# Query products of the second sequence: f32 replaced by three passes of split f32r parts that borrow the feed-forward's weight space

## The chip, the cores and the metric

One core of a Trainium2 chip runs the whole kernel. The metric is device time in microseconds of one execution, as the median of several runs. Times inside an execution come from the hardware profiler, counted from the first instruction. TensorE is called PE, VectorE DVE, ScalarE ACT, GpSimd POOL, and SyncE, which issues nearly all transfers, SP.

## The reference

Two transformer layers over two sequences of 512 rows of width 512, each layer an attention part and a feed-forward part with a layer norm behind each. What matters here is the attention of layer 0, a memory that is read, and the feed-forward behind it:

```python
q = (x @ Wq.T + bq).reshape(b, s, 32, 128)
q_sel = (elu(q) + 1.0)[:, :, ::4, :]                 # 8 heads are used
num = einsum('bshd,hde->bshe', q_sel, M)
den = einsum('bshd,hd->bsh', q_sel, z)[..., None] + 1e-6
out = repeat(num / den, 4, axis=2).reshape(b, s, 4096) @ Wo.T
x = layernorm(x + out)
# feed-forward of layer 0: weights that are ternary times a scale, width 1376
gate, up = (x / 128) @ w_gate.T, (x / 128) @ w_up.T
inter = trunc(clip(silu(gate) * up * 128, -128, 127))
x = layernorm(x + trunc(clip(inter @ w_down.T * 128, -128, 127)))
# layer 1: softmax attention with one head, then a gated feed-forward of width 1376
```

## The kernel before

Rows lie in eight tiles `xs[b][t]` of 128 rows, sequence b, tile t. Layer 0's attention goes in three stages on PE.

First, `queries(0, xt, h)` for eight heads: the rows of sequence 0 are transposed on PE (`first_rows`), and each head is four f32 products of 128x128 by 128x512 (`query_products`, L325). ACT takes the exponential (L361) and the positive part (L363) from PSUM, DVE joins them into `q` (L365).

Second, the rows of sequence 1 are transposed (`transposed`, L125) and `queries(1, xt1, h)` does the same for them. Between the heads lie the eight `fold(h)`: M and Wo of a head are multiplied in advance into `mw` (L387 to L390). The four parts of Wo that share a head are added first, by `sum_weights` (L380, L382), for heads 0, 3, 5, 7 on POOL and for the others on DVE. Column 511 of `mw` is `z`, so that one product gives both the numerator and the denominator.

Third, `read(b, t, ...)` for the eight row tiles: eight f32 products `po` (L401), a column `den` of each copied by ACT (L405), a reciprocal per four heads on DVE (L409). Three heads are scaled into `y` by ACT (L414) and added on POOL (L418), five are added to x on DVE (L423), and POOL adds the sum of the three (L427). Meanwhile the layer norm of the tile before is made: statistics on DVE, the root on POOL (L143, L144), `off` on DVE (L503), the application on ACT (L504).

In the same time the kernel proves that the feed-forward's weights are ternary. `check_up(c, a)` divides the gate (a = 0) or up half (a = 1) of chunk c by its scale into a tile `t` (ACT, L433) and compares it, multiplied again, with the weight (DVE, `compare`, L204). There are 22 of these; three follow each of the last five heads of sequence 1, and seven follow row tiles 0 to 2. `total` and `verdict` make a flag from the counts, on which PE branches at the start of the feed-forward. `divided(c, a)` (ACT, L433 too) writes the ternary weights `ts_up[c]` that the feed-forward multiplies with; chunks 0 to 2 are made during `read` and the rest in the feed-forward.

The weights come over SP's queue in program order: wq, x, m, wo, chunk 0, the rest of wo, chunks 1 to 10 (`gu`, 512 KB each, L237), wqkv, bqk, bv, wo1, bo (L310 to L315); a transfer that waits for its buffer holds back those queued after it. Only POOL keeps the program's order. The order on the other engines is found by a planner from priorities and its own estimate of costs; `tc.issue_after` forces an instruction behind another on its engine.

Layer 1 already multiplies in f32r with numbers split exactly into an upper part, a lower part and a difference (`row_parts`, `weight_parts`): three passes whose products are put together by ACT and DVE (`sum_up`, L1080 and L1081).

Of the kernel before, what the change touches and what calls it, by code (L numbers as in the profile page):

```python
# [19 lines left out]
P = 128  # L20
# [9 lines left out]
LAST = HID - 1  # L30
LENT = 3
# [5 lines left out]
def kernel(  # L37
# [34 lines left out]
    wqkv = const.tile([P, NK, 3 * D], F32, tag="wqkv", name="wqkv")  # L72
    bv = const.tile([P, D], F32, tag="bv", name="bv")
    wo1 = const.tile([D, HID], F32, tag="wo1", name="wo1")
    bo = const.tile([P, HID], F32, tag="bo", name="bo")
# [194 lines left out]

    wop = ctx.enter_context(tc.tile_pool(name="wop", bufs=6))
# [9 lines left out]
    with tc.tile_pool(name="a0w", bufs=1) as a0w, tc.tile_pool(name="a0", bufs=2) as a0:  # L281
# [27 lines left out]
        gus += up_weights(gu0_in, "0", range(1, len(CHUNKS)))  # L309
        nc.sync.dma_start(wqkv, wqkv_in.rearrange("(k p) f -> p k f", p=P))  # L310
        bqk = const.tile([D, 3], F32, tag="bqk", name="bqk")
        nc.sync.dma_start(bqk, bqk_in)
        nc.sync.dma_start(bv, bv_in.to_broadcast([P, D]))
        nc.sync.dma_start(wo1, wo1_in)
        nc.sync.dma_start(bo, bo_in.to_broadcast([P, HID]))  # L315
# [4 lines left out]
        mw = a0w.tile([D, NH, HID], F32, tag="mw", name="mw")  # L320
        nc.gpsimd.tensor_copy(mw[:, :, LAST], z)

# [8 lines left out]
        def first_rows(xt, t):  # L331

            pt = psum(f"pt_a00_{t}")
            for k in range(NK):
                done = nc.tensor.transpose(pt[:, ts(k, P)], xs[0][t][:, ts(k, P)], ident)
            pt = pt.rearrange("p (k t) -> p k t", k=NK)
            nc.scalar.copy(xt[:, :2, ts(t, P)], pt[:, :2])
            nc.vector.tensor_copy(xt[:, 2:, ts(t, P)], pt[:, 2:])
            return done

        def first_queries(pq, xt):

            done = first_rows(xt, 0)
            for t in range(NT):
                if t + 1 < NT:
                    with tc.issue_after(done.ins):
                        done = first_rows(xt, t + 1)
                with tc.issue_after(done.ins):
                    done = query_products(pq, xt, 0, ts(t, P))
            return done  # L350

        def queries(b, xt, h):

            pq = psum(f"pq_{b}_{h}")
            if b == h == 0:
                done = first_queries(pq, xt)
            else:
                done = query_products(pq, xt, h, slice(0, S))

            e = a0.tile([D, S], F32, tag="e", name=f"e_{b}_{h}")  # L360
            nc.scalar.activation(e, pq, AF.Exp, bias=bq[:, h : h + 1])  # L361
            r = a0.tile([D, S], F32, tag="r", name=f"r_{b}_{h}")
            nc.scalar.activation(r, pq, AF.Relu, bias=bq[:, h : h + 1])  # L363
            q = a0.tile([D, S], F32, tag="q", name=f"q_{b}_{h}", bufs=16)
            nc.vector.scalar_tensor_tensor(q, e, 1.0, r, ALU.min, ALU.add)  # L365
            qs[b].append(q)
            return done
# [17 lines left out]
        def fold(h):  # L385
            p = psum(f"pmw_{h}")
            nc.tensor.matmul(p, m[:, h, :], wos[h], start=True, stop=True)  # L387
            c = small.tile([P, 1], F32, tag="col", name=f"col_{h}", bufs=2)
            nc.scalar.mul(c, p[:, LAST:], -1.0)
            nc.scalar.activation(mw[:, h, :LAST], p[:, :LAST], AF.Identity, bias=c)  # L390

        def read(b, t, between):
# [3 lines left out]
            for h0 in range(0, NH, 4):  # L396
                four = []
                den = small.tile([P, 4], F32, tag="den", name=f"den_{b}_{t}_{h0}")
                for j in range(4):
                    po = psum(f"po0_{b}_{t}_{h0 + j}")  # L400
                    nc.tensor.matmul(  # L401
                        po, qs[b][h0 + j][:, ts(t, P)], mw[:, h0 + j, :],
                        start=True, stop=True,
                    )
                    nc.scalar.activation(  # L405
                        den[:, j : j + 1], po[:, LAST:], AF.Identity, bias=den_eps
                    )
                    four.append(po)
# [29 lines left out]

        def check_up(c, a):
            n = CHUNKS[c][1]  # L440
            w = gus[c][:, a].rearrange("p k i -> p (k i)")
            t = a0.tile([P, NK * P], F32R, tag="t", name=f"t_{c}_{a}")
            ternary(nc.scalar, t[:, : NK * n], w, inv_up[:, a : a + 1])
# [8 lines left out]
        qs = [[], []]  # L452
        xt = xtp.tile([P, NK, S], F32, tag="xt", name="xt_a00")
        with tc.issue_after(queries(0, xt, 0).ins):
            queries(0, xt, 1)
        for h in range(2, NH):
            queries(0, xt, h)
            if h == 4:
                sum_weights(nc.gpsimd, 0)
                turn_memory()  # L460
                sum_weights(nc.vector, 1)
            elif h == 6:
                xt1 = transposed(xs[1], "a01")
                sum_weights(nc.vector, 2)
        sum_weights(nc.gpsimd, 3)
        for h in range(NH):
            queries(1, xt1, h)
            if h == 0:
                sum_weights(nc.vector, 4)
                sum_weights(nc.gpsimd, 5)  # L470
                fold(0)
                fold(1)
                mx_up = largest(
                    [gus[0][:, a].rearrange("p k i -> p (k i)") for a in range(2)], "up"
                )
# [15 lines left out]
            if h >= 3:  # L491
                for _ in range(3):
                    check_up(*checks.pop(0))
        order = [(b, t) for b in range(B) for t in range(NT)]
# [11 lines left out]
        def divided(c, a):  # L506
            n = CHUNKS[c][1]
            if c not in ts_up:
                t = query_tile(f"tu_{c}").bitcast(F32R)
                ts_up[c] = t.rearrange("p a (k i) -> p a k i", k=NK)  # L510
                if n < P:
                    nc.gpsimd.memset(ts_up[c][:, :, :, n:].bitcast(F32), 0.0)
            ternary(nc.scalar, ts_up[c][:, a, :, :n], gus[c][:, a], inv_up[:, a : a + 1])

        ts_up, x2 = {}, []
        for i, (b, t) in enumerate(order):
            steps = read(b, t, lambda steps: norm_a0(i - 1, steps) if i else None)
            for _ in range((3, 2, 2, 0, 0, 0, 0, 0)[i]):
                check_up(*checks.pop(0))
            if i == 3:  # L520
                tot_up = total(counts, "up")
            elif i == 4:
                flag_up, eff_up = verdict(tot_up, sc_up, "up")
            if i in (3, 4, 5):
                for a in range(2):
                    divided(i - 3, a)
# [23 lines left out]
    with tc.tile_pool(name="f0", bufs=2) as f0:  # L550
# [52 lines left out]
        to_divide = [(c, a) for c in range(3, len(CHUNKS)) for a in range(2)]  # L603
# [71 lines left out]
        to_divide[2:2] = [None, None]  # L675
# [73 lines left out]

    BIG = 4096.0
    MAIN, CROSS = 1.0 + 1.0 / BIG, 1.0 / BIG
    UPPER = 1.0 - 2.0**-13
    cutp = ctx.enter_context(tc.tile_pool(name="cutp", bufs=2))  # L760

    def upper(h, src):
        return nc.scalar.activation(h, src, AF.Copy, scale=UPPER)
# [16 lines left out]
    def row_parts(src, parts):  # L780

        h, l, d = parts
        upper(h, src)
        nc.vector.tensor_sub(l, src, h.bitcast(F32))
        return nc.vector.scalar_tensor_tensor(
            d, l.bitcast(F32), -BIG, h.bitcast(F32), ALU.mult, ALU.add
        )

# [5 lines left out]

    def units(tile):
        return [tile[:, i, :] for i in range(tile.shape[1])]
# [28 lines left out]
    early = inter_tiles("early", F32R)  # L825
    room0 = units(early[0][2]) + units(early[1][2])
    room1 = units(early[0][1]) + units(early[1][1])
# [453 lines left out]
```

## Time and profile before

| what | us |
|---|---|
| median of 3 runs (471.8 to 799.53) | 472.01 |
| the profiled execution | 471.99 |
| its span, first to last instruction | 470.0 |
| PE busy | 463.0 |
| DVE busy | 327.9 |
| ACT busy | 268.1 |
| POOL busy | 114.4 |

The granted TensorE clock was 0.996 of full speed. Busy times of an engine overlap where its instructions are pipelined: a record's length is more than the step from one start to the next. The mean load of an engine over the span says little here, since the stages load the engines differently.

### The profile page before, as it was taken

The page shows a single profiled execution, that of the slowest core. Times are in us where ns is not written, and L with a number is a line of the kernel's source. Part 1 is how long each engine was busy: PE and PEld are TensorE (multiplying, and loading weights), DVE is VectorE, ACT ScalarE, POOL GpSimd, SP SyncE. Part 2 cuts the span into 40 slices and gives each one's busy share as a digit, 9 for nine tenths or more (in the row PEclk, how much of TensorE's full clock was granted, in tenths as well). Part 3 has the DMA queues.
Part 4 walks back from the last instruction along what each step waited for, and adds up shares of the span by engine and source line. Part 5 has one row for each costly group of instructions (what it writes and reads, how often), then busy time and mean ns, then how long its engine had stood idle before and what let it go on. Part 6 is the DMA issues. An engine that isn't in the chain of part 4 may idle for free.

```text
span 470.0 us, 5725 instructions
## 1 busy us (share of the span) xinstructions
PE 463.0 (99%) x1899; PEld 330.7 (70%) x1899; DVE 327.9 (70%) x622; ACT 268.1 (57%) x507; POOL 114.4 (24%) x141
## 2 busy tenths in 40 slices
PE   9999999999999999999999999999999999999995
PEld 8454444434478788888866568888888888888885
DVE  1265677767857677755988989986666767998633
ACT  3344799557556877645756743575644768532201
POOL 0343101566460090400348032000000000041101
PEclk9999999999999999999999999999999999999998
DMA  8999800000015000213192000000000000001011
GB/s 311 373 348 382 301 2 0 0 0 3 1 54 188 3 1 1 92 47 81 58 360 94 0 1 1 1 0 1 1 0 1 0 1 1 1 24 45 22 46 45
DMA packets 15187, 33.97 MB, mean 72 GB/s; under 512 B 3440, under 2 KB 4336, under 8 KB 15152
## 3 DMA queue, kind: packets, MB, share of 16 engines
q1 hardware_dynamic: 14864, 33.14, 19.6%
q8 instruction: 22, 0.36, 0.3%
q10 hardware_dynamic: 288, 0.36, 0.2%
q14 instruction: 13, 0.11, 0.1%
HBM read 31.40 MB, written 2.10 MB: 71 GB/s over the span
## 4 chain that ended last, share of the span: by engine, by line
PE 72%; ACT 7%; DVE 5%; issue 3%; POOL 0%; POOLq 0%; DVEq 0%; ACTq 0%
PE pm L1071 17%; PE pg_f L567 9%; PE pu_f L567 8%; PE pc L1071 8%; PE pdm L1159 7%; PE pd_f L622 4%; PE pdc L1159 4%; DVE x L423 4%; PE pqk L853 3%; PE po L401 2%; ACT y L414 2%; ACT t L433 2%; PE pv L866 2%; PE pot L949 1%; PE po L965 1%
## 5 line engine op out<-in xcount | busy, mean ns | idle before, releaser
L401 PE MATMUL po<-mw,q 128*128 128x512 f32 x128 | 57.1, 598 | 0.3 <-DVE mv_a L137 0.2
L325 PE MATMUL pq<-xt_a,wq 128*128 128x512 f32 (+1 forms) x152 | 56.9, 526 | 0.0
L143 POOL TENSOR_TENSOR rstd_f<-mv_f,ln_eps 128x1 f32<-128x1 f32 x15 | 4.4, 295 | 172.1 <-DVE mv_f L1174 130.2
L401 PEld LDWEIGHTS po<-mw,q 128*128 128x128 f32 x128 | 23.0, 189 | 32.1 <-issue 17.7
L325 PEld LDWEIGHTS pq<-xt_a,wq 128*128 128x128 f32 x152 | 26.2, 190 | 27.3 <-issue 26.2
L1071 PE MATMUL pm<-r,ugu 128*128 128x512 f32 x152 | 37.7, 389 | 0.0
L1071 PE MATMUL pm<-r,it_early 128*128 128x512 f32 x144 | 36.7, 392 | 0.0
L1071 PEld LDWEIGHTS pm<-r,ugu 128*128 128x128 f32 x152 | 28.5, 188 | 5.9
L1071 PEld LDWEIGHTS pm<-r,it_early 128*128 128x128 f32 x144 | 27.0, 188 | 6.0 <-issue 0.5
L423 DVE SCALAR_TENSOR_TENSOR x<-po,den,x 128x511 f32<-128x511 f32 x40 | 29.8, 745 | 1.9
L165 ACT ACTIVATE ta_f<-y_f,below_half 128x512 int8<-128x512 f32 (+1 forms) x22 | 15.9, 723 | 23.7 <-DVE y_f L155 23.3
L1081 DVE SCALAR_TENSOR_TENSOR ev_q<-pm,ev_q 128x512 f32<-128x512 f32 x27 | 18.6, 687 | 14.1 <-PE pm L1071 14.1
L418 POOL TENSOR_TENSOR y<-y,y 128x511 f32<-128x511 f32 x16 | 20.3, 1272 | 31.5 <-ACT y L414 30.8
L593 DVE SCALAR_TENSOR_TENSOR it_f<-tb_f,ta_f 128x512 fp32r<-128x512 int16 (+1 forms) x22 | 15.2, 690 | 16.3 <-ACT tb_f L166 16.3
L361 ACT ACTIVATE e<-pq,bq 128x512 f32<-128x512 f32 x16 | 11.1, 691 | 24.1 <-PE pq L325 21.7
L567 PE MATMUL pg_f<-xh,tu 128*128 128x512 f32 x88 | 24.7, 401 | 0.0
L1080 ACT ACTIVATE ev_q<-pc 128x512 f32<-128x512 f32 x27 | 16.0, 594 | 14.1 <-PE pc L1071 14.0
L435 POOL TENSOR_SCALAR td<-wd,inv_down 128x512 fp32r<-128x512 f32 x11 | 18.6, 1710 | 22.0 <-DVE inv_down L199 22.0
L567 PE MATMUL pg_f<-xl,tu 128*128 128x512 f32 x88 | 23.6, 390 | 0.0
L567 PE MATMUL pu_f<-xh,tu 128*128 128x512 f32 x88 | 23.6, 389 | 0.0
L567 PE MATMUL pu_f<-xl,tu 128*128 128x512 f32 x88 | 23.5, 389 | 0.0
L961 ACT ACTIVATE x<-x,off_f,rstd_f 128x512 f32<-128x512 f32 x7 | 5.7, 816 | 27.7 <-POOL off_f L960 27.7
(310 smaller groups left out, 1088.3 us busy)
## 6 DMA issues: line engine op xcount, KB each, us to landing
gu<-in_gu SPq DMA_DIRECT2D x20, 512.0 KB, 8.0
wo<-in_wo SPq DMA_DIRECT2D x16, 512.0 KB, 5.7
wd<-in_wd SPq DMA_DIRECT2D x20, 256.0 KB, 4.9
wq<-in_wq SPq DMA_DIRECT2D x8, 256.0 KB, 4.1
x<-in_x SPq DMA_DIRECT2D x7, 256.0 KB, 4.4
out<-x SPq DMA_DIRECT2D x7, 256.0 KB, 2.0
wqkv<-in_wqkv SPq DMA_DIRECT2D x1, 768.0 KB, 10.7
m<-in_m SPq DMA_DIRECT2D x1, 512.0 KB, 5.8
```

The source lines that it names most:

```text
L165: nc.scalar.activation(a[:n], y, AF.Relu, bias=below_half[:n])
L325: done = nc.tensor.matmul(pq[:, at], wq[h][:, k, :], xt[:, k, at], start=(k == 0), stop=(k == NK - 1),)
L401: nc.tensor.matmul(po, qs[b][h0 + j][:, ts(t, P)], mw[:, h0 + j, :], start=True, stop=True,)
L418: nc.gpsimd.tensor_add(ys[0][:, :LAST], ys[0][:, :LAST], y[:, :LAST])
L423: steps.append(nc.vector.scalar_tensor_tensor(x[:, :LAST], four[j][:, :LAST], d, x[:, :LAST], ALU.mult, ALU.add))
L435: eng.tensor_scalar(out, w, factor, None, ALU.mult)
L567: nc.tensor.matmul(pp[a], t[:, a, i % NK, :], x2[b][i], start=(i == 0), stop=(i == 2 * NK - 1),)
L622: nc.tensor.matmul(pd, inter[b][c][:, ts(t, P)], td[c].bitcast(F32R), start=(c == 0), stop=(c == last),)
L1071: nc.tensor.matmul(p, w, x, start=(left[id(p)] == begun[id(p)]), stop=(left[id(p)] == 1))
L1080: nc.scalar.activation(ev, pc, AF.Copy, scale=CROSS)
L1081: nc.vector.scalar_tensor_tensor(ev, pm, MAIN, ev, ALU.mult, ALU.add)
L1159: nc.tensor.matmul(p[:, :w], got[j // 4][1][kind][:, j % 4], down_parts[j][kind][:, cols], start=(j == 0 and kind == kinds[0]), stop=(j == ...
```

## The change

The query products of sequence 1 no longer run in f32. `second_rows(k)` transposes a block of rows as before and makes three f32r parts of it from PSUM: the upper part and its multiple by 4096 on ACT, the lower part and the difference on DVE. `split_query(h)` makes the three parts of a head's weights with `row_parts` (one ACT, two DVE operations). `second_queries(h)` then runs four f32r products into one PSUM bank (`pc`) and eight into another (`pm`); ACT and DVE put them together in `both`, and the ELU is made from that: an exponential on ACT, a `tensor_scalar` and a two-input operation on DVE.

The parts need room. The weights' parts lie in the buffers of chunks 1 to 9 of the feed-forward's weights, in the second half of `mw`, which is now two tiles `mws`, and for head 7 in a buffer of `xtp`. The rows' parts lie in `xtp`, in the `y` buffers and in the space of wqkv, wo1 and bo. So chunks 1 to 9 are loaded one after the other behind heads 1 to 6 of sequence 1 (`done_with`), and wqkv, bqk, bv, wo1 and bo after head 7.

The checks move: two follow each of heads 4 to 7, and fourteen follow row tiles 0 to 5. For chunks 0 to 3 the check's division is the one of `divided`, made once and kept. For chunks 4 to 10 the division of the up half runs on POOL. `total` and `verdict` come two row tiles later. `BIG`, `MAIN`, `CROSS`, `UPPER`, `upper`, `row_parts` and `units` are moved ahead unchanged, and the f32r tiles that layer 1 called `early` are called `spare`.

```diff
@@ tiles @@
+    early = [const.tile([P, 3, 512], F32R, tag="wqkv", name="e_wqkv")]
...
+    early += [const.tile([P, 1, 512], F32R, tag=tag, name=f"e_{tag}") for tag in ("wo1", "bo")]
@@ attention of layer 0 @@
-        gus += up_weights(gu0_in, "0", range(1, len(CHUNKS)))
-        nc.sync.dma_start(wqkv, wqkv_in.rearrange("(k p) f -> p k f", p=P))
+        gus += [None] * (len(CHUNKS) - 1)
+
+        def load_up(*chunks):
+            for c, gu in zip(chunks, up_weights(gu0_in, "0", chunks)):
+                gus[c] = gu
...
-        mw = a0w.tile([D, NH, HID], F32, tag="mw", name="mw")
-        nc.gpsimd.tensor_copy(mw[:, :, LAST], z)
+        room = [a0w.tile([P, 4, 512], F32R, tag="mw1", name="wp_mw")]
+        room = units(room[0])[:3]
+        for c in range(1, 10):
+            room += units(wffn.tile([P, 2, 512], F32R, tag=f"gu{c}", name=f"wp_{c}"))
+        wq_parts = [room[i : i + 3] for i in range(0, len(room), 3)]
+        done_with = {1: (1,), 2: (2, 3), 3: (4,), 4: (5, 6), 5: (7,), 6: (8, 9)}
+
+        def split_query(h):
+            with tc.issue_after(copies[2 * NT - 2].ins), tc.issue_after(copies[2 * NT - 1].ins):
+                row_parts(wq[h].rearrange("p k d -> p (k d)"), wq_parts[h])
+
+        def second_rows(k):
+            pt = psum(f"pt_a01_{k}")
+            for t in range(NT):
+                turned = nc.tensor.transpose(pt[:, ts(t, P)], xs[1][t][:, ts(k, P)], ident)
+            hx, l, d = x_parts[k]
+            upper(hx, pt)
+            big = a0.tile([P, S], F32, tag="t", name=f"hb_{k}")
+            nc.scalar.activation(big, hx.bitcast(F32), AF.Copy, scale=BIG)
+            nc.vector.scalar_tensor_tensor(l, pt, BIG, big, ALU.mult, ALU.subtract)
+            rows_done.append(nc.vector.tensor_sub(d, l.bitcast(F32), hx.bitcast(F32)))
+            return turned
+
+        def second_queries(h):
+            u, l, d = (w.rearrange("p (k d) -> p k d", k=NK) for w in wq_parts[h])
+            pc, pm = psum(f"pqc_{h}"), psum(f"pqm_{h}")
+            for k in range(NK):
+                nc.tensor.matmul(
+                    pc, d[:, k], x_parts[k][2], start=(k == 0), stop=(k == NK - 1)
+                )
+            for k in range(NK):
+                for i, w in enumerate((u, l)):
+                    nc.tensor.matmul(
+                        pm, w[:, k], x_parts[k][i],
+                        start=(k == i == 0), stop=(k == NK - 1 and i == 1),
+                    )
+            both = a0.tile([D, S], F32, tag="r", name=f"r_1_{h}")
+            nc.scalar.activation(both, pc, AF.Copy, scale=CROSS)
+            nc.vector.scalar_tensor_tensor(both, pm, MAIN, both, ALU.mult, ALU.add)
+            e = a0.tile([D, S], F32, tag="e", name=f"e_1_{h}")
+            nc.scalar.activation(e, both, AF.Exp, bias=bq[:, h : h + 1])
+            q = a0.tile([D, S], F32, tag="q", name=f"q_1_{h}", bufs=16)
+            nc.vector.tensor_scalar(q, both, bq[:, h : h + 1], 0.0, ALU.add, ALU.max)
+            nc.vector.scalar_tensor_tensor(q, e, 1.0, q, ALU.min, ALU.add)
+            qs[1].append(q)
...
         def check_up(c, a):
...
-            t = a0.tile([P, NK * P], F32R, tag="t", name=f"t_{c}_{a}")
-            ternary(nc.scalar, t[:, : NK * n], w, inv_up[:, a : a + 1])
+            if c < DIVIDED:
+                divided(c, a)
+                t = ts_up[c][:, a].rearrange("p k i -> p (k i)")
+            else:
+                t = a0.tile([P, NK * P], F32R, tag="t", name=f"t_{c}_{a}")
+                eng = nc.gpsimd if a else nc.scalar
+                ternary(eng, t[:, : NK * n], w, inv_up[:, a : a + 1])
...
+        for h in range(4):
+            split_query(h)
...
         for h in range(2, NH):
-            queries(0, xt, h)
+            done = queries(0, xt, h)
+            if h >= 5:
+                with tc.issue_after(elus[h - 1].ins):
+                    split_query(h - 1)
+            if h < 4:
+                for k in range(2):
+                    with tc.issue_after(done.ins):
+                        done = second_rows(2 * h - 4 + k)
             if h == 4:
                 sum_weights(nc.gpsimd, 0)
                 turn_memory()
-                sum_weights(nc.vector, 1)
+                with tc.issue_after(rows_done[-1].ins):
+                    sum_weights(nc.vector, 1)
             elif h == 6:
-                xt1 = transposed(xs[1], "a01")
-                sum_weights(nc.vector, 2)
+                with tc.issue_after(rows_done[-1].ins):
+                    sum_weights(nc.vector, 2)
         sum_weights(nc.gpsimd, 3)
+        load_up(10)
+        wq_parts.append(units(xtp.tile([P, NK, 512], F32R, tag="xt", name="wp_xt"))[:3])
         for h in range(NH):
-            queries(1, xt1, h)
+            second_queries(h)
+            load_up(*done_with.get(h, ()))
             if h == 0:
+                split_query(7)
                 sum_weights(nc.vector, 4)
                 sum_weights(nc.gpsimd, 5)
+                half_of_products()
...
-            if h >= 3:
-                for _ in range(3):
+            if h >= 4:
+                for _ in range(2):
                     check_up(*checks.pop(0))
+        wqkv = const.tile([P, NK, 3 * D], F32, tag="wqkv", name="wqkv")
+        nc.sync.dma_start(wqkv, wqkv_in.rearrange("(k p) f -> p k f", p=P))
...
         for i, (b, t) in enumerate(order):
             steps = read(b, t, lambda steps: norm_a0(i - 1, steps) if i else None)
-            for _ in range((3, 2, 2, 0, 0, 0, 0, 0)[i]):
+            for _ in range((2, 3, 2, 3, 2, 2, 0, 0)[i]):
                 check_up(*checks.pop(0))
-            if i == 3:
+            if i == 5:
                 tot_up = total(counts, "up")
-            elif i == 4:
+            elif i == 6:
                 flag_up, eff_up = verdict(tot_up, sc_up, "up")
-            if i in (3, 4, 5):
-                for a in range(2):
-                    divided(i - 3, a)
```

## The prediction

> **What bounds the kernel now.** I read the page's busy shares first, then TensorE's (PE's) order of time around the query products, then the order of time of VectorE (DVE), ScalarE (ACT) and GpSimd (POOL) in the stage behind them, then the table by stage. The page:
>
> ```profile
> span 470.0 us, 5725 instructions
> PE 463.0 (99%) x1899; PEld 330.7 (70%) x1899; DVE 327.9 (70%) x622; ACT 268.1 (57%) x507; POOL 114.4 (24%) x141
> ```
>
> PE is busy from end to end, so what counts is how many microseconds PE's own list takes, and where it is held back without looking idle. PE in order of time (start, length, line), second sequence's query products and the stages behind:
>
> ```profile
> 42.51 3.60 PE L325 MATMUL pq<-xt_a,wq 128*128 128x512 f32 x8
> 45.95 0.27 PE L184 MATMUL pmx_up<-ident,mx_up 128*2 128x128 f32 x1
> ...
> 68.88 3.60 PE L325 MATMUL pq<-xt_a,wq 128*128 128x512 f32 x8
> 72.31 35.47 PE L401 MATMUL po<-mw,q 128*128 128x512 f32 x80
> ...
> 130.65 1.50 PE L567 MATMUL pg_f<-xh,tu 128*128 128x512 f32 x4
> ```
>
> One head in f32 is eight records, and the next starts 3.44 us on (45.95 less 42.51). The stage that reads the memory (`read`, L401) runs from 72.31 to 130.65, 58.34 us. Its 64 f32 products are 0.86 us each (3.44 / 4), so 55.0, and 16 transposes add 1.74 (0.87 per eight records at L264): 56.8. So 1.5 us of that stage is PE being held. What holds it shows on DVE, one tile of rows:
>
> ```profile
> 91.94 0.20 DVE L503 TENSOR_SCALAR off<-mv_a,rstd_a 128x1 f32<-128x1 f32 x1
> 92.06 0.17 DVE L409 RECIPROCAL den<-den 128x4 f32<-128x4 f32 x1
> 92.34 0.75 DVE L423 SCALAR_TENSOR_TENSOR x<-po,den,x 128x511 f32<-128x511 f32 x1
> 95.36 0.18 DVE L409 RECIPROCAL den<-den 128x4 f32<-128x4 f32 x1 [2.28 <-ACT den L405]
> ...
> 99.27 0.20 DVE L503 TENSOR_SCALAR off<-mv_a,rstd_a 128x1 f32<-128x1 f32 x1
> 99.39 0.17 DVE L409 RECIPROCAL den<-den 128x4 f32<-128x4 f32 x1
> ```
>
> It is a loop of two engines: the reciprocal at 92.06 releases ACT (norm 0.7, three y, four den: 3.3 us), ACT releases the reciprocal at 95.36, DVE adds four heads and the statistics (4.0 us), and so on: 7.33 us a tile against PE's 6.87. In it DVE has one hole, the 2.28 us before 95.36 (2.13 in later tiles). POOL in the same tile:
>
> ```profile
> 92.11 1.27 POOL L427 TENSOR_TENSOR x<-x,y 128x511 f32<-128x511 f32 x1 [0.80 <-DVE x L423]
> 94.22 2.61 POOL L418 TENSOR_TENSOR y<-y,y 128x511 f32<-128x511 f32 x2 [0.85 <-ACT y L414]
> ```
>
> POOL works 4.6 us of 7.3 here, 3.9 of them tensor_tensor.
>
> **What the skill says.** The Trainium skill, SBUF — State Buffer, "Who interferes with whom": a DVE instruction with two SBUF inputs contends with a GpSimd instruction that reads SBUF, and the one that comes second waits for the whole of the first. The trace agrees for POOL's tensor_tensor:
>
> ```profile
> 25.27 1.21 DVE L380 TENSOR_TENSOR wo<-wo,wo 128x1024 f32<-128x1024 f32 x1
> 30.87 2.05 DVE L380 TENSOR_TENSOR wo<-wo,wo 128x1024 f32<-128x1024 f32 x1 [2.58 <-DMA wo<-in_wo]
> 30.58 1.26 POOL L382 TENSOR_TENSOR wos<-wo 128x512 f32<-128x512 f32 x1
> ```
>
> (first two from DVE, third from POOL): the second add takes 0.84 us more, until POOL ends at 31.84. Against POOL's tensor_scalar it agrees less: of eleven compares `junk_d` beside or near L435 the median is 0.75 and the worst 1.17 us. VectorE: DVE Perf Modes, "The perf-mode tier table": f32 tensor_scalar in SBUF has a 2× mode and two-input operations have none; here L155 takes 0.43 us, the two-input L593 0.69.
>
> **The change, part by part.** Back to back, a two-input DVE operation of 128x512 costs 0.61 us (starts of L365 and L380's neighbours at 26.41, 27.01, 27.61), an ACT pass 0.61, a compare 0.85 (75.77 to 76.61, its accumulator read included), a tensor_scalar 0.35.
>
> (1) PE. Removed: eight heads at 3.44 = 27.5. Added: eight heads of twelve single-pass products. The feed-forward runs eight such in 1.81 us and the twelve of the second layer's up product at 2.72 (the chain's 311.66 to 314.38); the weight load is 0.19 and fits in 0.227. 8 x 2.72 = 21.8. Saved: **5.75 us**. The 16 transposes of the second sequence move forward between heads 2 and 4 and stay 16. x of the second sequence is issued at 7.5 to 9.4 us and lands some 4.4 later, before head 2 ends at about 17.5, so the move costs 0.
>
> (2) Splits. Rows: four blocks of two ACT and two DVE operations, in place of four copies. Weights: eight heads of one ACT and two DVE. DVE stands idle for 2.25, 2.74 and 5.57 us between 10 and 22 us, and works 11.4 of 16.4 us from 24.4 to 40.8. Seven heads and the rows need 22 x 0.61 = 13.4, less two copies, 12.2; heads 0 to 3 and the rows (9.8) fall in the first hole. Cost 0. The adds of folded weights wait behind `rows_done` by perhaps 2 us; `fold` 2 and 3, the next users, come at about 47. If that cover went, PE would wait up to 2.
>
> (3) Second query stage. It begins on PE at 37.4 (33.93 + 3.44) and now lasts 21.8 + eight folds 6.9 + 0.4 = 29.1, to 66.5. DVE there: 8 x (0.61 + 0.35 + 0.61) = 12.6, eight compares 6.8, the rest of two sums 2.4, splits 2.4, small 0.8: 25.0, plus some 2 us of waits behind POOL's two sums (7.6 us long in all). 27 of 29: late, not over. ACT: eight passes for `pc`, eight exponentials, eight folds of 0.8, eight ternaries, one split: 21.6 of 29, where it was full before (8.60 of 8.60 from 56.0 to 64.6). Cost 0, bound 0 to 2.
>
> (4) Loads. SP now issues weight chunks 1 to 9 one by one behind heads 1 to 6, then wqkv, bqk, bv, wo1 and bo. Each waits for that head's products with everything on SP queued behind it. Chunks 8 and 9 go out near 61 us and need about 8 us at worst (the page's median of a full queue); tile 3 uses them near 90. wqkv is used at 236, wd is issued at 137.7 anyway. Cost 0.
>
> (5) Checks in `read`. Seven of 22 compares were left for this stage; now 14 are, in tiles 0 to 5 as 2, 3, 2, 3, 2, 2. From chunk 4 on, POOL forms the ternary of every second one: 1.70 us (L435, eight in 13.61), behind POOL's x add and ahead of its next y adds. A compare has two SBUF inputs; POOL holds tensor_tensor 3.9 of 7.3 us, so on the mean it waits 0.53 x 0.65 = 0.35: 1.2 us each. One of the fourteen falls in the long lead of tile 0 (5.85 us from 72.31 to the first reciprocal at 78.16); 13 x 1.2 = 15.6 against six holes of 2.2 = 13.2. Over: 2.4, all of it in the loop. Tile 3 has two POOL ternaries: 4.6 + 3.4 = 8.0 against 7.3, 0.7. Together **3.1 us given back**. Bounds: if every compare finds a hole, 0, and then PE's own 56.8 can also take back up to 1.5; if they fall badly, see rival B. POOL ternary beside a compare: between 0 and 0.4 of extra wait by L204's rows; I take 0.
>
> (6) ACT loses the six `divided` of tiles 3 to 5 and two later. In the trace they ran by 82 us, off the loop. 0. The verdict moves from tile 4 to 6, near 120; the branch needs it near 128. 0, at most 1 if PE reaches the sum first.
>
> Sum: -5.75 + 3.1 = -2.65. The profiled execution took 471.99 us, span 470.0 and 2.0 around it; the median of the runs is 472.01. 472.0 - 2.65 = **469.3 us**.
>
> **Rivals.** A, the full gain (0.2): the holes take everything. For it: five compares ran between 75.8 and 83 without stretching tiles 0 and 1 (7.17 and 6.73 us). Against: three on a tile need 2.55 of 2.2. 472.0 - 5.75 = 466.3.
>
> B, slower (0.3): POOL's ternary ends near 95.05 (93.4 + 1.65), just when the hole closes, and POOL's waiting y add starts at once. A compare set ahead of the reciprocal of 95.36 waits for that add until 96.35 and ends at 97.1: the loop is 1.75 us later. Six tiles make 10.5, net +4.75: 476.7. It decides from 3.3 such tiles (5.75 / 1.75). For it: POOL's list has this order. Against: the reciprocal and adds are older work, and a compare issued after them falls in the next hole.
>
> C, nothing gained (0.1): DVE becomes the bound of the query stage: 27 of 29 with more waits behind POOL, and banks fill. 2 us there plus the 3.1: 471.4.
>
> **How the numbers follow.** The forecast's own case has 0.4, from 467.5 to 471.5. The range 465.8 to 477.5 reaches from A with a little of the held 1.5 to B and leaves out some 2 in 10. Two per cent, 9.4 us, is about what a measurement of this kernel can tell from no change. A faster run by that needs more than the whole PE saving: 0.01. A slower one needs 15 given back, B on every tile together with C: 0.06. Same 0.93.
>
> **What would show it.** Right: query stage of eight heads at 2.72 spacing; first L401 product near 66.5; tile period on DVE 7.3 to 8; ends of read near 128. Wrong: compares with 1.5 us and more ahead of the second reciprocal of a tile (B), PE gaps between heads of the second sequence with DVE as releaser (C), or a start of read later than 68.

## The result, and the profile after

The changed kernel takes 496.09 us in the median, against 472.01 before: ratio 1.051, 95% interval 1.049 to 1.052. It is slower by 24.1 us, where 469.3 was predicted. The profiled execution took 496.01 us, its span 494.2. The page of the changed kernel, its engine shares, and two of its costliest groups (busy time and mean ns of one; then idle time ahead of them and who ended most of it):

```profile
PE 464.9 (94%) x1931; PEld 338.5 (68%) x1931; DVE 362.1 (73%) x660; ACT 267.4 (54%) x506; POOL 129.7 (26%) x149
...
L490 PE MATMUL po<-mw,q 128*128 128x512 f32 x128 | 60.7, 620 | 12.1 <-DVE x L512 11.3
...
L205 DVE SCALAR_TENSOR_TENSOR junk<-t,sc_up,gu 128x512 int8<-128x512 f32 (+1 forms) x14 | 18.6, 1328 | 14.0 <-POOL t L524 13.6
```

PE was busy 99% of the time and is now 94%. The compares of the later chunks (L205) average 1.33 us, and DVE stands idle for 13.6 us waiting for POOL's ternary (L524). PE's order of time, second query stage and the stage that reads the memory:

```profile
46.42 0.27 PE L185 MATMUL pmx_up<-ident,mx_up 128*2 128x128 f32 x1 [1.83 <-DVE mx_up L178]
...
55.23 0.58 PE L196 MATMUL pbc_up<-dg_up,ones 2*128 2x2 f32 x2 [5.78 <-DVE dg_up L189]
55.74 3.78 PE L475 MATMUL pmw<-wos,m 128*128 128x512 f32 x4
...
76.75 17.33 PE L490 MATMUL po<-mw,q 128*128 128x512 f32 x40
95.23 1.10 PE L490 MATMUL po<-mw,q 128*128 128x512 f32 x2 [1.15 <-DVE x L512]
...
105.41 1.12 PE L490 MATMUL po<-mw,q 128*128 128x512 f32 x2 [2.32 <-DVE x L512]
...
127.24 5.59 PE L490 MATMUL po<-mw,q 128*128 128x512 f32 x8 [3.99 <-DVE x L512]
...
154.43 1.48 PE L687 MATMUL pg_f<-xh,tu 128*128 128x512 f32 x4
```

The reader sees PE held in two places. From the starts of the first products of each stage:

| stage (us) | before | predicted | after | after less before |
|---|---|---|---|---|
| start of the second query stage | 37.4 | 37.4 | 36.8 | -0.6 |
| second query stage | 34.9 | 29.1 | 40.0 | +5.0 |
| `read` | 58.3 | 61.4 | 77.7 | +19.3 |
| everything behind | 339.4 | 339.4 | 339.8 | +0.4 |

**The read stage.** DVE in one of its tiles (start, length, line; idle time ahead and its releaser at the end):

```profile
98.08 0.17 DVE L498 RECIPROCAL den<-den 128x4 f32<-128x4 f32 x1
98.35 0.75 DVE L512 SCALAR_TENSOR_TENSOR x<-po,den,x 128x511 f32<-128x511 f32 x1
100.99 1.75 DVE L205 SCALAR_TENSOR_TENSOR junk<-t,sc_up,gu 128x512 int8<-128x512 f32 x1 [1.89 <-POOL t L524]
...
102.84 1.57 DVE L205 SCALAR_TENSOR_TENSOR junk<-t,sc_up,gu 128x512 int8<-128x512 f32 x1
...
104.33 0.17 DVE L498 RECIPROCAL den<-den 128x4 f32<-128x4 f32 x1
```

and POOL beside it:

```profile
98.12 1.28 POOL L516 TENSOR_TENSOR x<-x,y 128x511 f32<-128x511 f32 x1 [0.78 <-DVE x L512]
99.38 1.58 POOL L524 TENSOR_SCALAR t<-gu,inv_up 128x512 fp32r<-128x512 f32 x1
100.92 2.94 POOL L507 TENSOR_TENSOR y<-y,y 128x511 f32<-128x511 f32 x2
```

DVE is free from 99.10. The ternary stands on POOL behind the x add and ends at 100.96. The compare starts at 100.99, just as POOL's first y add has taken hold, and takes 1.75 us in place of 0.75. The second compare meets the second y add: 1.57. Only then does the reciprocal run, at 104.33, 6.25 us behind the first one; before, it was 3.30 (95.36 less 92.06). So this pair of compares (the up half of one chunk, whose ternary is POOL's, and the gate half of the next, whose ternary is ACT's) costs the loop 2.95 us. The tile period says nearly the same: second reciprocals at 94.06, 104.33 and 114.59, 10.26 us apart where they were 7.33. Seven chunks (4 to 10) at 2.93 would be 20.5 us. The later tiles are less even: the next two periods, the first of them with two POOL ternaries, are 11.58 and 9.13 us. The whole is measured below. Of the 2.95, as worked out from these rows: two undisturbed compares of 0.85 begun at 100.99 would end at 102.69, which is 1.3 later than 101.38, when the reciprocal was due. That is the late start; the other 1.64 is the wait for the two adds. The tile with two POOL ternaries holds a control. There POOL's next instruction behind the first ternary is the second ternary and not a y add, and both compares take 0.75 us:

```profile
119.89 1.58 POOL L524 TENSOR_SCALAR t<-gu,inv_up 128x512 fp32r<-128x512 f32 x1
122.36 2.10 POOL L524 TENSOR_SCALAR t<-gu,inv_up 128x512 fp32r<-128x512 f32 x1 [0.89 <-DVE junk L205]
...
121.51 0.75 DVE L205 SCALAR_TENSOR_TENSOR junk<-t,sc_up,gu 128x512 int8<-128x512 f32 x1 [2.16 <-POOL t L524]
...
122.36 0.75 DVE L205 SCALAR_TENSOR_TENSOR junk<-t,sc_up,gu 128x512 int8<-128x512 f32 x1
```

Behind each of the other six ternaries come the y adds, and the compare that each of these ternaries releases takes 1.61 to 1.75 us.

**The query stage.** It is 10.9 us longer than the 29.1 of the working. Two waits make 7.6 of it (1.83 and 5.78 above). A third part comes on top: PE's four records at 55.74 take 3.78 us where four such took 1.88 to 1.98 before. The windows of the changed kernel show why (stretch; length; busy time of PE, weight loads, DVE, ACT, POOL; then PE's clock, the DMA share and GB/s):

```profile
49.00:50.00 1.00, 0.45 (x3) 0.03 (x1) 1.00 (x3) 0.28 (x1) 0.64 (x1) 1.00 0.70 270
...
53.00:54.00 1.00, 0.00 (x0) 0.00 (x0) 1.00 (x3) 0.00 (x0) 0.00 (x0) 0.50 0.11 41
...
58.00:59.00 1.00, 1.00 (x3) 0.34 (x1) 1.00 (x2) 1.00 (x3) 0.00 (x0) 0.50 0.00 0
59.00:60.00 1.00, 1.00 (x3) 0.55 (x2) 0.82 (x3) 0.39 (x2) 0.33 (x1) 0.60 0.00 0
```

PE stops at 49.45 and its clock falls to 0.50 at 53.0. It comes back at about 59.8 (0.60 in the last row is four fifths of it at 0.50 and one at 1.00), 4.6 us after PE began to work again at 55.23. Half of 4.6, an estimate of what this cost, is 2.3 us. The waits and this make 9.9 of the 10.9; the last 1.0 is not traced. The Trainium skill, TensorE: Matmul & The Clock Gate, Part 1, states this: half clock after about 3.4 us idle, full clock after about 3.4 us of work. The trace has 3.5 and 4.6 here. But a shorter wait, in `read`, halved the clock too:

```profile
145.22 0.56 PE L218 MATMUL pf_up<-tot_up,ones 128*128 128x1 f32 x2 [2.56 <-DVE tot_up L211]
```

The clock was 0.50 from about 145.1 to 148.5 us. So 3.4 us is no safe limit in this kernel; a wait of 2.56 us was enough.

What PE waits for at 55.23 is the scale, and DVE's order shows why that is late:

```profile
42.62 0.68 DVE L178 TENSOR_REDUCE mx_up<-gu 128x1 f32<-128x512 f32 x1
43.21 2.46 DVE L291 SCALAR_TENSOR_TENSOR wp<-wp,wp 128x512 fp32r<-128x512 f32 x1
45.60 0.67 DVE L178 TENSOR_REDUCE mx_up<-gu 128x1 f32<-128x512 f32 x1
...
49.62 2.64 DVE L291 SCALAR_TENSOR_TENSOR wp_xt<-wp_xt 128x512 fp32r<-128x512 f32 x1
...
54.97 0.21 DVE L189 TENSOR_SCALAR dg_up<-ident,top_up 2x2 f32<-2x2 f32 x1
```

From 39.67 to 57.14 its rows follow one another without a hole. Two splits in that list are stretched from 0.69 to 2.46 and 2.64 us by POOL's weight sums:

```profile
42.74 2.39 POOL L468 TENSOR_TENSOR wo<-wo,wo 128x1024 f32<-128x1024 f32 x1 [9.68 <-DVE wp L290]
...
49.36 2.35 POOL L468 TENSOR_TENSOR wo<-wo,wo 128x1024 f32<-128x1024 f32 x1 [1.43 <-DMA wo<-in_wo]
```

### The profile page after: what moved, and what is told of

Read it like the earlier page. It is cut to its first block, busy times and chain, and to the rows that moved or that the text cites. A ratio compares the mean times of both kernels' runs of the same rounds, so it can differ in the third digit from the quotient of the medians.

```text
span 494.2 us, 5863 instructions
## 1 busy us (share of the span) xinstructions
PE 464.9 (94%) x1931; PEld 338.5 (68%) x1931; DVE 362.1 (73%) x660; ACT 267.4 (54%) x506; POOL 129.7 (26%) x149
## 4 chain that ended last, share of the span: by engine, by line
PE 65%; DVE 5%; issue 3%; POOL 3%; ACT 1%; POOLq 0%; DVEq 0%
PE pm L1165 16%; PE pg_f L687 8%; PE pu_f L687 8%; PE pc L1165 8%; PE pdm L1253 7%; PE pdc L1253 4%; PE pqk L947 3%; PE po L490 1%; DVE x L512 1%; PE pv L960 1%; PE pot L1043 1%; PE po L1059 1%; PE psc L985 1%; POOL t L524 1%; DVE junk L205 1%
## 5 line engine op out<-in xcount | busy, mean ns | idle before, releaser
L490 PE MATMUL po<-mw,q 128*128 128x512 f32 x128 | 60.7, 620 | 12.1 <-DVE x L512 11.3
L512 DVE SCALAR_TENSOR_TENSOR x<-po,den,x 128x511 f32<-128x511 f32 x40 | 29.8, 745 | 1.8
L494 ACT ACTIVATE den<-po,den_eps 128x1 f32<-128x1 f32 x64 | 14.6, 267 | 30.3 <-PE po L490 30.3
L205 DVE SCALAR_TENSOR_TENSOR junk<-t,sc_up,gu 128x512 int8<-128x512 f32 (+1 forms) x14 | 18.6, 1328 | 14.0 <-POOL t L524 13.6
L411 PE MATMUL pq<-xt_a,wq 128*128 128x512 f32 (+1 forms) x88 | 28.7, 478 | 0.0
L507 POOL TENSOR_TENSOR y<-y,y 128x511 f32<-128x511 f32 x16 | 22.1, 1383 | 24.0 <-ACT y L503 23.3
L713 DVE SCALAR_TENSOR_TENSOR it_f<-tb_f,ta_f 128x512 fp32r<-128x512 int16 (+1 forms) x22 | 15.2, 690 | 16.3 <-ACT tb_f L167 16.3
L524 POOL TENSOR_SCALAR td<-wd,inv_down 128x512 fp32r<-128x512 f32 x11 | 18.6, 1710 | 22.5 <-PE pbc_down L196 22.5
L411 PEld LDWEIGHTS pq<-xt_a,wq 128*128 128x128 f32 x88 | 14.1, 191 | 11.7 <-issue 11.2
```

Of the source, the lines that this page charges most:

```text
L205: nc.vector.scalar_tensor_tensor(junk, t, sc, w, ALU.mult, ALU.not_equal, accum_out=count)
L411: done = nc.tensor.matmul(pq[:, at], wq[h][:, k, :], xt[:, k, at], start=(k == 0), stop=(k == NK - 1),)
L490: nc.tensor.matmul(po, qs[b][h0 + j][:, ts(t, P)], mws[h0 // 4][:, j, :], start=True, stop=True,)
L507: nc.gpsimd.tensor_add(ys[0][:, :LAST], ys[0][:, :LAST], y[:, :LAST])
L512: steps.append(nc.vector.scalar_tensor_tensor(x[:, :LAST], four[j][:, :LAST], d, x[:, :LAST], ALU.mult, ALU.add))
L524: eng.tensor_scalar(out, w, factor, None, ALU.mult)
```

## The experiments

All ratios are to the kernel before, with 95% intervals.

**Ternary on ACT.** Theory: POOL's ternary costs the read stage its time. One line of the changed kernel:

```diff
-                eng = nc.gpsimd if a else nc.scalar
+                eng = nc.scalar
```

> The changed kernel with one line different: the check's division of chunks 4 to 10 runs on ACT for both halves, none on POOL. Theory (the pair of compares waits for POOL's ternary, which follows the x add, and then for two y adds[...]): the stage of the row tiles shrinks from 77.7 us to 60 to 63, and the run to 478 to 482. Rival (the mere number of compares on DVE in that stage is too high): the stage stays above 72 us and the run above 489.

Measured 477.69 us, ratio 1.010 (1.006 to 1.014): 18.4 us come back. PE's order of time in this kernel:

```profile
78.56 10.46 PE L490 MATMUL po<-mw,q 128*128 128x512 f32 x24
89.78 31.48 PE L490 MATMUL po<-mw,q 128*128 128x512 f32 x72 [0.76 <-ACT den L494]
...
137.62 1.50 PE L687 MATMUL pg_f<-xh,tu 128*128 128x512 f32 x4
```

`read` takes 59.1 us, and the waits for `x L512` are gone. The line moves more than the ternary, though. POOL keeps the program's order and ACT does not have to: the last compare now starts at 90.83 us, where it started at 142.71. So the run shows what the ternary on POOL costs in all, and not how much of that is the collision and how much the late place. (The query stage ended at 78.56 here, 1.8 us later.)

**The checks alone, on the kernel before.** No splits, no passes: only the layout of the checks. (The six separate divisions of chunks 0 to 2 stay on ACT.)

```diff
-            ternary(nc.scalar, t[:, : NK * n], w, inv_up[:, a : a + 1])
+            eng = nc.gpsimd if a and c >= 4 else nc.scalar
+            ternary(eng, t[:, : NK * n], w, inv_up[:, a : a + 1])
...
-            if h >= 3:
-                for _ in range(3):
+            if h >= 4:
+                for _ in range(2):
...
-            for _ in range((3, 2, 2, 0, 0, 0, 0, 0)[i]):
+            for _ in range((2, 3, 2, 3, 2, 2, 0, 0)[i]):
...
-            if i == 3:
+            if i == 5:
...
-            elif i == 4:
+            elif i == 6:
```

> The kernel before, f32 query products and early loads kept, with only the layout of the checks taken over: two behind each of heads 4 to 7, fourteen behind row tiles 0 to 5, up halves of chunks 4 to 10 divided on POOL. Theory: the row tile stage grows from 58.3 to 73 to 78 us and the run to 486 to 492, without any split. Rival (the stage suffers because the query stage hands over late, or from the splits): within 4 us of the kernel before.

Measured 490.80 us, ratio 1.039 (1.035 to 1.042): 18.8 us are lost without any of the split passes. PE of this kernel:

```profile
73.58 17.33 PE L401 MATMUL po<-mw,q 128*128 128x512 f32 x40
92.06 1.10 PE L401 MATMUL po<-mw,q 128*128 128x512 f32 x2 [1.15 <-DVE x L423]
...
102.23 1.12 PE L401 MATMUL po<-mw,q 128*128 128x512 f32 x2 [2.31 <-DVE x L423]
...
142.02 0.35 PE L217 MATMUL pf_up<-tot_up,ones 128*128 128x1 f32 x2 [2.56 <-DVE tot_up L210]
...
151.30 1.49 PE L568 MATMUL pg_f<-xh,tu 128*128 128x512 f32 x4
```

`read` takes 77.7 us (151.30 less 73.58), as long as in the changed kernel. The first three waits (1.15, 2.31, 2.67) are those of the changed kernel within 0.01 us. It is the checks, and it does not need the new query stage.

**No checks in the read stage, and no compares at all.** Both start from the changed kernel. The first:

```diff
+        nc.gpsimd.memset(counts, 0.0)
...
         def check_up(c, a):
+            if c >= DIVIDED:
+                return
```

> The changed kernel without the 14 checks of chunks 4 to 10 (their ternary and compare are left out; the counts stay zero there), so that nothing but the normal work of the first and second engine is left in the read stage; the split passes, sums and the eight checks inside the query stage are as they were. Theory (the whole read-stage loss is these checks, the rest is the query stage): the query stage still ends at 75.5 to 77, the read stage takes 56 to 59 instead of 77.7, and the kernel comes to 474 to 478 us, ratio 1.005 to 1.013. Rival (the split passes shift work of the read stage as well): read stage over 62, over 480 us.

Measured 475.77 us, 1.0075 (1.0054 to 1.0095). The query stage still ends at 77.03, and `read` takes 57.5:

```profile
77.03 41.36 PE L490 MATMUL po<-mw,q 128*128 128x512 f32 x96
...
134.56 1.49 PE L690 MATMUL pg_f<-xh,tu 128*128 128x512 f32 x4
```

So the stage without these checks takes 57.5 us, and the 14 checks as laid out cost 77.7 less 57.5, 20.2 us. That is 2.9 us a chunk on the mean of the seven.

The second leaves out the eight compares of the query stage as well and keeps their divisions on ACT:

> As the run without read-stage checks, and the eight compares of chunks 0 to 3 are left out too (their ternaries on ACT stay). Theory that the query stage is late because of splits, sums and weight loads and not because of its checks: its end moves from 76.8 by no more than 2 us, to 74.5 to 76, kernel 473 to 477 us. Rival that the checks between its evictions pace it: it ends below 72, kernel under 471 us.

Measured 476.20 us, 1.009 (1.006 to 1.013). The query stage ends at 76.53. Its own eight compares are not what makes it late.

**What makes the query stage late: the held sum.** The ternary on ACT, and the sum of head 1 no longer behind `rows_done`.

```diff
-                with tc.issue_after(rows_done[-1].ins):
-                    sum_weights(nc.vector, 1)
+                sum_weights(nc.vector, 1)
```

> As e1_ternary_act, and the sum of head 1's output weights on DVE no longer waits for the row parts. Theory (that gate holds buffers, delays the loads of wo by 6 to 9 us and so DVE and then PE in the query stage): 4 to 6 us less than e1_ternary_act, read stage begins at 71 to 73 us. Rival (DVE simply has too much work there, and two-input operations wait for POOL's sums): less than 1.5 us from e1_ternary_act.

Measured 474.38 us, 1.0055 (1.0034 to 1.0076): 3.3 us less than with the ternary on ACT alone, somewhat under what was expected; `read` begins at 74.27 us in place of 78.56, where 71 to 73 was expected. The link is the load queue. Issues of the changed kernel, then of this one (start and length of the stretch of issues):

```profile
32.79 12.69 SPq L333 DMA_DIRECT2D wo<-in_wo  x7
45.59 28.36 SPq L238 DMA_DIRECT2D gu<-in_gu  x9
```

```profile
32.85 7.33 SPq L333 DMA_DIRECT2D wo<-in_wo  x5
```

The pool of the output weights `wo` has six buffers, and a sum frees two. With the sum held, the last of `wo` went out at 45.5; here at 40.2; before, at 36.4.

**The scale moved, and two POOL sums left out.** Both start from the kernel with the ternary on ACT and the sum not held. First, the two small products of the scale go behind heads 3 and 4:

```diff
-            elif h == 1:
-                top_up = over_partitions(mx_up, "up")
             elif h == 2:
-                sc_up, inv_up = scales(top_up, "up")
                 fold(2)
             elif h == 3:
                 fold(4)
+                top_up = over_partitions(mx_up, "up")
+            elif h == 4:
+                sc_up, inv_up = scales(top_up, "up")
```

> As e3_act_sum_free, and the two small PE products of the scale (pmx, pbc) stand two heads later, behind heads 3 and 4. Theory (PE, which keeps its order, stands still for 1.8 and 5.8 us only because these two wait for DVE's late list, and then runs at a lower clock): the query stage has no gap over 1 us, read begins at 66.5 to 69 us, run 465 to 470. Rival (DVE's lateness comes out elsewhere, as full PSUM banks): read begins at 73 or later, run within 2 us of e3_act_sum_free.

Measured 476.58 us, 1.010 (1.007 to 1.013): 2.2 us more, so that theory fell. PE's wait moved instead, to 1.71 us at a fold and 2.56 at the scale, and the stage ended at 73.95 against 74.27. DVE's list was still full up to 52.6 us; the place where PE runs into it had changed. PE's clock halved all the same, from 61.9 to 65.3 us, behind the wait of 2.56. `read`, with the checks later, took 60.9 us against 59.0.

> As e3_act_sum_free, but the sums of the output weights of heads 5 and 7 on POOL are left out (the first of the four parts is used unsummed), so the output differs. Theory (DVE is late in the query stage because its two-input operations, splits, sums and ELU, wait for POOL's tensor_tensor; in e3_act_sum_free such waits are some 2.1, 1.8 and 0.6 us from 37 to 47): DVE's rows of 2 us and more are gone after 34 us, read begins 4 to 6 us earlier than in e3_act_sum_free (74.3), run 468.5 to 470.5. Rival (DVE's own number of operations): read begins less than 1.5 us earlier, run within 1.5 us of e3_act_sum_free.

(The sums of heads 5 and 7 return their first part unsummed.) Measured 472.56 us, 1.000 (0.998 to 1.002): 1.8 us less in the medians (the two profiled spans differ by 0.6). PE's wait for the scale fell from 4.54 to 2.80, but `read` began at 73.78 us, only 0.5 earlier, where the theory asked for 4 to 6. By the stage's end the rival, DVE's own number of operations, fits better: on this base the two sums on POOL are a small part of the delay.

**The splits early, with and without the later scale.** On the same base, heads 4 to 6 are split together with 0 to 3:

```diff
-        for h in range(4):
+        for h in range(7):
             split_query(h)
...
-            if h >= 5:
-                with tc.issue_after(elus[h - 1].ins):
-                    split_query(h - 1)
```

> As e3_act_sum_free, but the weights of heads 4, 5 and 6 are split at once with those of heads 0 to 3, not behind the ELU of heads 4, 5 and 6. Theory (DVE is late because six operations were put into its fullest part while it stood idle for 5.5 us before 21.8): they fit there at no cost, DVE is 3.6 to 6 us earlier with the maxima and the scale, the two gaps of PE shrink to under 2 us in all, read begins at 68 to 71 us, run 467 to 471. Rival (POOL's sums and loads of wo set DVE's pace, not the number of operations): read begins at 73 or later, run within 1.5 us of e3_act_sum_free.

Measured 476.14 us, 1.009 (1.006 to 1.011). It was meant to empty the second half of DVE's list and gained nothing: 1.8 us more, and the stage ended at 75.38, 1.1 later.

> As e8_splits_early, and the two small PE products of the scale stand behind heads 3 and 4 as in e6_scale_later. Theory (with DVE no longer late the position doesn't matter for PE, and later scale means checks spill into the row tiles): within 2 us of e8_splits_early, more likely slower. Rival (PE still waits for the scale in e8_splits_early): 2 to 4 us faster, run 464.5 to 467.5.

This is the one above with the later scale. Measured 475.18 us, 1.008 (1.005 to 1.010), and POOL's first sum shows what early splits can cost:

```profile
18.33 4.52 POOL L468 TENSOR_TENSOR wo<-wo,wo 128x1024 f32<-128x1024 f32 x1 [10.53 <-DMA wo<-in_wo]
```

It took 2.36 us in the changed kernel. Now DVE's two-input operations, back to back from before it began until 20.63 us, hold up POOL. DVE later stands 4.99 us, until 42.76, waiting for `wo`. That the one leads to the other is not shown: without the later scale the same sum ran in 2.36 us, from 19.97, and DVE still stood 4.93 us, until 42.92.

**No weight sum on POOL.** All eight `sum_weights` on DVE, on top of the early splits:

```diff
-                sum_weights(nc.gpsimd, 0)
+                sum_weights(nc.vector, 0)
...
-        sum_weights(nc.gpsimd, 3)
+        sum_weights(nc.vector, 3)
...
-                sum_weights(nc.gpsimd, 5)
+                sum_weights(nc.vector, 5)
...
-                sum_weights(nc.gpsimd, 7)
+                sum_weights(nc.vector, 7)
```

> As e8_splits_early, but all eight sums of output weights run on DVE and none on POOL. Theory (the query stage is late because DVE's two-input operations and POOL's sums hold each other up, which frees the wo buffers late, so that the last wo loads go out at 42 to 46 us instead of 36, and DVE stands in front of them): no DVE row over 1.3 us from 18 to 50, last wo load by 37 us, read begins at 67 to 70 us, run 466 to 470. Rival (DVE's sheer work, now 7 us more, is the bound): read begins at 76 us or later, run 477 or more.

Measured 473.15 us, 1.001 (0.999 to 1.003), query stage to 73.08. Against the early splits with the sums shared (476.14 us, 75.38), the pair in which only the engine of the sums differs, that is 3.0 us less. The expected 67 to 70 was not reached. No DVE row from 18 to 50 us is over 1.3 us now, though DVE has more work, but the last `wo` goes out at 42.3 us, not by 37. The single runs spread from 468.73 to 474.81 us, with PE's clock from 0.998 down to 0.990. With the later scale on top:

> As e11_sums_dve, with the scale's two small PE products behind heads 3 and 4. Theory: PE's gap before the scale is gone as well, read begins at 66.5 to 69 us, run 464.5 to 468; the checks come later and cost up to 1.5 us in the row tiles. Rival (DVE's work is the bound): within 1.5 us of e11_sums_dve and above 475.

Measured 471.44 us, 0.9985 (0.9971 to 0.9999), stage to 70.57, where 66.5 to 69 was expected. The move that gained nothing by itself is worth 1.7 us here (1.0 us, within the spread, with early splits and the sums shared). What is left stands in DVE's order of this kernel:

```profile
40.48 1.22 DVE L468 TENSOR_TENSOR wo<-wo,wo 128x1024 f32<-128x1024 f32 x1 [3.88 <-DMA wo<-in_wo]
```

**The same, splits where the change has them.** Sums then come ahead of the splits of heads 4 to 6 in DVE's list.

> The changed kernel with the ternary on ACT, sum of head 1 not held back, no weight sum on POOL, the scale behind heads 3 and 4, and the rows of heads 4 to 6 split where the change put them (behind the first sequence's queries), instead of at once. Theory (sums ahead of splits free the weight buffers earlier): last load of wo issued before 40 instead of 42, query stage ends at 69 to 70.5 instead of 70.6, 470 to 471.4 us. Rival (splits late crowd the start of the second query stage): it ends at 71 to 73, 472 to 474 us.

Measured 470.12 us, ratio 0.996 (0.995 to 0.997): 0.4% under the kernel before, a small but clear gain, and far under the changed one. The last `wo` goes out at 39.6, and PE's order of time is:

```profile
44.11 0.39 PE L378 MATMUL pqc<-e_wqkv,wp 128*128 128x512 f32 x1
...
46.83 1.88 PE L475 MATMUL pmw<-wos,m 128*128 128x512 f32 x4
...
56.58 0.35 PE L196 MATMUL pbc_up<-dg_up,ones 2*128 2x2 f32 x2 [1.37 <-DVE dg_up L189]
...
67.83 10.46 PE L490 MATMUL po<-mw,q 128*128 128x512 f32 x24
...
78.70 1.10 PE L490 MATMUL po<-mw,q 128*128 128x512 f32 x2 [0.41 <-ACT t L522]
...
128.75 1.49 PE L686 MATMUL pg_f<-xh,tu 128*128 128x512 f32 x4
```

One head is 2.72 us (46.83 less 44.11). The query stage takes 31.4 us, from 36.46, and `read` 60.9. Its windows (columns as above):

```profile
36.80:66.00 29.20, 27.83 (x109) 19.77 (x108) 26.87 (x52) 19.11 (x38) 0.58 (x1) 1.00 0.59 197
```

DVE is busy 26.9 of 29.2 us, POOL 0.6, PE 27.8, with a full clock.

## Why the prediction was wrong

The predicted stages, 29.1 and 61.4 us, are within 2.3 us of those of this last kernel, and its time of 470.1 is close to the 469.3 predicted. What was forecast is thus near to what the query passes do when POOL shares neither the sums nor the ternaries, the held sum is free and the scale comes later. That the totals meet is in part luck: the forecast's 3.1 us in `read` were for compares that wait for POOL, and in that kernel the first waits of PE in `read` name ACT's ternary (0.41 us above). The kernel as changed shares both, and the failing steps are those that priced the sharing. Of the 26.8 us between forecast and result, 16.3 lie in step (5) and 10.9 in step (3); the start came 0.6 earlier.

(1) PE's saving: right. 2.72 us a head was measured.

(5) Checks in `read`, 3.1 us: the step that failed, by 16 us. It took the wait of a compare behind POOL as a mean, share of POOL's held time times half an add, 0.35 us. The wait isn't random. POOL's list is in order, and the ternary that releases the compare is directly ahead of the y adds, so the release and the collision are one event. The compares measured 1.75 and 1.57 instead of 1.2, and they began 1.9 us into a hole of 2.28, so the hole did not absorb them. Rival B had the mechanism, place and direction, but counted one compare and 1.75 us a tile. The gate half of the next chunk, whose ternary is ACT's, also came after POOL's, since DVE keeps its order, and the price was 2.95 for such a pair, 2.9 on the mean of seven chunks. The sub-step that a POOL ternary beside a compare costs DVE nothing has one row for it, the compare of 0.75 us at 122.36. Its reading of the kernel before was mixed: of the eleven compares `junk_d` only six run while POOL works on L435 (163.41 to 177.02 and 188.90 to 193.90 us), and three of these took 1.00, 1.17 and 1.02 us.

(3) Query stage, "27 of 29: late, not over", cost 0: failed by 10.9 us. The load was summed over the stage, but it isn't spread over it. Splits, sums, maxima and evictions fill DVE from 39.67 to 57.14 without a hole, and the scale's small operations, for which PE's in-order list waits, stand at the end of that list. The two POOL sums held two splits for about 1.9 us each, where 2 in all was set; how much of the 10.9 us that makes is open, since without these two sums the stage ended only 0.5 us earlier on the base tried above. Rival C named this bound and priced it at 2 us. No term was there for PE's half clock after the wait, about 2.3 us.

(2) Splits, cost 0, "adds of folded weights wait behind `rows_done` by perhaps 2 us": failed. The sum of head 1 began at 27.4 instead of 21.9, 5.5 us later. The step asked only when the sum's user comes, and not what the sum frees: two of six buffers, and behind them the loads. Freeing it gave 3.3 us.

(4) Loads, cost 0: nothing seen against it. The chunk loads went out late, from 45.59 us, but the compares of `read` waited for POOL's ternary. SP's order was not quite the stated one: bqk and bv went out at 31.79 and 32.26 us, ahead of the last seven of `wo`, not after head 7.

(6) ACT and verdict, at most 1: in the changed kernel PE waits 2.56 us at `pf_up` for it, as it does with the checks alone (142.02 above). With the ternary on ACT no such wait shows. It is a consequence of the late checks, and is in the stage's 77.7 us.

One reading in the prediction is loose, though no sum rests on it: the rows set beside the tier table are not the f32 case, since L155 works on int32 and L593 has an int16 input.

Not tried: POOL's ternary at another place in POOL's list. So the division of the 2.95 us into late start (1.3) and lock (1.64) is arithmetic on one tile. How much of the 18.4 us another place on POOL would return stays open. Nor were the sums moved to DVE by themselves in the changed kernel, so how the gain from 74.27 to 67.83 us in the query stage divides between the sums and the later scale is not shown.

## What to carry to other kernels

Before a mean wait is charged for a shared resource, look at what releases the waiting instruction: if the releaser's next instruction on its engine is the one that holds the resource, expect the collision every time and not on the mean (here six of six). A stage's load divided by its length says nothing where a small operation at the end of an in-order list gates PE; walk the list up to that operation instead. And of an instruction that is held back, price the buffers it frees, not only the value it makes.

## What the hardware showed that was not expected

PE's clock was 0.50 from 53.0 to about 59.8 us, around one wait of 5.78 us, and by the estimate above the wait so cost 2.3 us more than its length. A wait of 2.56 us halved the clock as well.

The lock between DVE and POOL works in both directions. DVE's split took 2.64 us beside a POOL add, against 0.69. POOL's add took 4.52 us beside DVE's splits, against 2.36, and was held through several of them. This agrees with the Trainium skill, SBUF — State Buffer, "Who interferes with whom", that the order of issue decides who waits. With a one-input operation on POOL it goes both ways too: the ternary that began together with a compare at 122.36 was stretched to 2.10 us, from 1.58, and the compare kept its 0.75, while in the kernel before three compares beside such operations took 1.00 to 1.17 us.

Moving all eight sums to the busier engine did not lengthen the query stage. With only that changed it ended at 73.08 us against 75.38. In the last kernel above, with DVE at 27 of 29 us and POOL nearly empty, it ran in 31.4 us, against 40.0 with the sums shared, though there the place of the scale and the held sum were changed as well.
